# Seven places per dense tile, and a node's own row by a one on the counts' diagonal

## The chip, the cores and the metric

The kernel runs on one core of a Trainium2 chip. The metric is the device time of one execution in microseconds (us). A core has five engines that run their own instruction streams in order and wait for each other by semaphores: TensorE (PE, with its weight loads shown apart as PEld), VectorE (DVE), ScalarE (ACT), GpSimd (POOL) and SyncE (SP, which issues DMAs).

## The reference

The program is one block of a graph network on 6250 nodes with 256 features and 200000 edges, sorted by destination. Cut to what matters here:

```python
xn = _layernorm(x)
# graph convolution: self-loops and symmetric norm
src, dst = concat([A[0], loop]), concat([A[1], loop])     # loop = arange(N): every node's own row
deg  = segment_sum(ones, dst);  dinv = rsqrt(deg)
h    = xn @ W
gnn  = relu(segment_sum(h[src] * (dinv[src] * dinv[dst])[:, None], dst) + b)
# linear attention over all nodes, layer norm, two-layer MLP, layer norm
x = x + gnn + mix(xn)
# top-1 routing to 8 experts with a capacity of 977 tokens, two-layer MLP each
x = x + ffn(_layernorm(x))
```

What bears on the change is the segment sum: for every node the rows of its neighbours, and its own row, are added up.

## The kernel before

The nodes lie in 49 tiles of 128. A first stage (to about 250 us) normalises x, makes the table of rows `h * dinv` (kept on chip as 49 tiles of 128 x 512, a high part and a rest of 256 columns each, and in memory as `g_dram`) and finds the edge lists. The last stage (from about 1150 us) is the experts' MLP. Between them lies the stage that the change rewrites. It runs under an order written out by hand: every engine executes its instructions in the order in which the program writes them. Three generators are stepped in turn.

**Dense tiles (`dense`, letter d).** For 32 of the tiles (`DTS`) the sum over neighbours is a full matrix product: a matrix A of 6272 x 128 counts (how many edges go from each source node to each destination) is multiplied with the whole table. A tile goes through three steps:

1. *Counts.* The tile's destinations are cut into 44 groups of three nodes (the last four groups: two nodes). For each group VectorE makes two one-hot matrices in bf16, `lo` (128 edges x 128 low parts of the source) and `hi` (128 edges x 147 columns, 49 blocks of three nodes), in `onehots` (L1134). TensorE multiplies them (L1177) into a PSUM bank `bp`, and ScalarE writes the bank as bytes into `A` (L1181; the narrow groups by L1184).
2. *Widening.* ScalarE widens some of the 49 source blocks of A to f32r, into `A_r` (L1165, `widened`). `A_r` has two buffers.
3. *The product.* TensorE multiplies every block with its table tile (L1199) and adds all up in one bank `ps_d`. Two products come first: an identity with the tile's own table rows (L1195, the self-loop), and `ohl` with the few left-over edges (L1196). ScalarE and VectorE put the sum away (`put_sum` L1121, `put_rest` L1126).

A tile has `half = NG // 4 = 11` places. In place p the product of tile u-1 takes a tenth of the blocks (p from 1), the one-hots of place p+1 of tile u are made, the next tenth is widened, and the counts of place p-1 are multiplied (four groups in two banks, L1177) and evicted (two evictions). In place 0 there is no product; in place 1 the counts come first.

**Gathered tiles (`gather`, letter g).** For the other 17 tiles the edges' rows are gathered from memory by GpSimd, 128 at a time (L1230, 561 gathers, nine buffers), and summed by a one-hot product (L1256) into `ps`. VectorE makes those one-hots `oh` four steps ahead (L1245), `ohg` once a tile (L1242).

**Rounds (`rounds`, letter s).** Everything else on a pair of tiles: attention, norms, MLP, and three rounds later routing. A plan puts each operation into a numbered slot: `at(k, f, ...)`. A round has `SLOTS_A_ROUND = 14` slots, and successive rounds overlap. Seven operations take one of three PSUM banks named `mm` (`bank()`, pool `mps` with three buffers): `attend` (L1453), `turn` (L295, as `mix_turn` and `slot_turn`), `first` (L1496), `second` (L1514), `gate` (L1422) and routing (L1311). A bank is given back by the operation that reads it: `attended` on VectorE (L1461 to L1466), `mix_turned` and `slot_turned` on ScalarE, `gelu` on ScalarE (L1504), `mixed`, `put_logits` and routing's next step on VectorE. With the pools of `ps` (2), `ps_d` (1) and `bp` (2) the eight banks are all given out.

The main loop steps them: one place of d, then as many slots of s as are due (about 1.01 per place), then as many steps of g as are due (about 1.6 per place). There are 33 x 11 = 363 places.

Of the kernel before, what the change touches and what calls it, by code (L numbers as in the profile page):

```python
# [8 lines left out]
BF16 = mybir.dt.bfloat16  # L9
# [46 lines left out]
SLOTS_A_ROUND = 14  # L56
S_RATE = 1.0104
S_LATE = 6
G_EARLY = 8
# [16 lines left out]
def graph_block_kernel(  # L76
# [127 lines left out]
    V.tensor_scalar(identr, jp, 0.0, None, op0=OP.is_equal)  # L204
    upto = const.tile([P, P], F32, name="upto")
# [12 lines left out]

    Z.tensor_scalar(upto, jp, 0.0, None, op0=OP.is_ge)
# [892 lines left out]
    with tc.manual_schedule():  # L1112
# [16 lines left out]
        def onehots(lists, p):  # L1129

            o = []
            for h, (name, row, w) in enumerate((("lo", rowb, P), ("hi", hib, HW))):
                one = de.tile([P, 4, w], BF16, name=name, tag=name, bufs=3)
                V.tensor_tensor(one.rearrange("p g (w t) -> p g w t", t=2),  # L1134
                                row.rearrange("p (w t) -> p w t", t=2).unsqueeze(1).to_broadcast([P, 4, w // 2, 2]),
                                lists[:, h, 4 * p:4 * p + 4, :].unsqueeze(2).to_broadcast([P, 4, w // 2, 2]),
                                op=OP.is_equal)
                o.append(one)
            return o

# [11 lines left out]
        def dense():  # L1152
# [3 lines left out]
            half = NG // 4  # L1156

            def share(p):
                return (p - 1) * NB // (half - 1), p * NB // (half - 1)

            def widened(u, p):

                s0, s1 = share(p)
                o = parts[p] = de.tile([P, 5, P], FR, name="A_r", tag="A_r")
                nc.scalar.copy(o[:, :s1 - s0, :], mats[u][:, s0:s1, :])  # L1165
# [3 lines left out]
            def counted():  # L1169
                if made and made[0][:2] < (u, p):  # L1170
                    uu, pp, (lo, hi) = made.pop(0)
                    for i in range(2):
                        g = 4 * pp + 2 * i
                        bp = bps.tile([P, 512], F32, name="bp", tag="bp")
                        both = bp[:, :2 * NB * GN].rearrange("p (s k) -> p s k", k=2 * GN)
                        for h in range(2):
                            nc.tensor.matmul(both[:, :, h * GN:(h + 1) * GN], lo[:, 2 * i + h, :],  # L1177
                                             hi[:, 2 * i + h, :NB * GN].rearrange("p (s k) -> p s k", k=GN),
                                             start=True, stop=True)
                        if g < NL:  # L1180
                            nc.scalar.copy(mats[uu][:, :, GN * g:GN * (g + 2)], both)  # L1181
                        else:
                            at = GN * NL + 2 * (g - NL)
                            nc.scalar.copy(mats[uu][:, :, at:at + 4].rearrange("p s (g k) -> p s g k", g=2),  # L1184
                                           both.rearrange("p s (g k) -> p s g k", g=2)[:, :, :, :2])

            for u in range(ND + 1):
                for p in range(half):
                    if p == 1:
                        counted()  # L1190
                    if u >= 1 and p >= 1:

                        if p == 1:
                            acc_ps = dps.tile([P, 2 * D], F32, name="ps_d", tag="ps_d")
                            nc.tensor.matmul(acc_ps, identr, source(DTS[u - 1]), start=True, stop=False)  # L1195
                            nc.tensor.matmul(acc_ps, ohl, left, start=False, stop=False)  # L1196
                        A, (s0, s1) = parts.pop(p), share(p)
                        for hi in range(s0, s1):
                            nc.tensor.matmul(acc_ps, A[:, hi - s0, :], source(hi), start=False, stop=(hi == NB - 1))  # L1199
# [10 lines left out]
                    if u >= 1 and 0 < p < half - 1:  # L1210
                        widened(u - 1, p + 1)
                    if u < ND and p == half - 3:
                        ohl = de.tile([P, P], FR, name="ohl", tag="ohl", bufs=1)
                        V.tensor_scalar(ohl, rowb, dsub[:, DTS[u]:DTS[u] + 1], None, op0=OP.is_equal)
# [5 lines left out]
                    if u >= 1 and p == 0:  # L1220
                        widened(u - 1, 1)
# [122 lines left out]
        def rounds():  # L1344
# [211 lines left out]
            for a in range(NGR):  # L1556
                k = S_ * a - (2 if a == NGR - 1 else 0)
                at(k - 9 if a else 0, load, a)
                at(k + 2, scaled, a)
                at(k + 2, attend, a, 0)  # L1560
                at(k + 4, attend, a, 1)
                at(k + 3, attended, a, 0)
                at(k + 5, attended, a, 1)
                at(k + 7, mix_stats, a, 0)
                at(k + 10, mix_norm, a, 0, (0, 1))
                at(k + 12, mix_turn, a)
                at(k + 13, mix_turned, a)
                at(k + 13, gained, a)
                k += S_
                at(k, first, a)  # L1570
                at(k + 1, gelu, a)
                at(k + 3, second, a)
                at(k + 4, mixed, a)
                if a == NGR - 1:
                    break
                at(k + (5 if a == NGR - 2 else 6), mix_stats, a, 2)
                at(k + 11, mix_norm, a, 2, (0, 1))
                at(k + 11, shift, a)
                at(k + 13, gain, a)
                at(k + 14, joined, a)  # L1580
            for c, r in takes.items():
                k = S_ * r - (2 if c == TAILC - 1 else 0)
                needs[k - 2] = c
                at(k - 2, add_bias, c)
                at(k + 1, to_slot, c)
                at(k + 2, slot_stats, c, 4)
                at(k + 12, slot_norm, c, 4)
                at(k + 13, slot_turn, c)
                at(k + 14, slot_turned, c)
                at(k + 15, gate, c)  # L1590
# [9 lines left out]
                at(k + 16, put_logits)  # L1600
                if c % 2:
# [5 lines left out]
                    at(k + 17, begin)  # L1607
                    soon = (18, 19, 19, 21, 21, 22, 23, 23, 24, 24)
                    sooner = (18, 22, 23, 24, 25, 26, 27, 27, 28, 28)
                    for d in soon if c == TAILC - 1 else sooner if c == TAILC - 3 else (18, 24, 25, 27, 28, 29, 30, 30, 31, 32):  # L1610
                        at(k + d, lambda c=c: walk(batches[c - 1][1]))
            for r in range(NGR):
                at(S_ * r + (6 if r == NGR - 1 else 8), start_roots)
                at(S_ * r + (7 if r == NGR - 1 else 9), end_roots)
# [60 lines left out]
            needs[z + 15], needs[z + 17], needs[z + 25] = b1, b0, b2  # L1675
            for k, f, *args in (
                    (10, enough),
                    (15, add_bias, b1), (15, to_sum, b1, 4),
                    (16, mix_stats, last, 2), (17, add_bias, b0), (17, to_sum, b0, 0),
                    (18, start_roots), (19, end_roots),  # L1680
                    (20, mix_norm, last, 2, (0, 1)), (20, filled, b1, 4), (21, filled, b0, 0),
                    (22, stored, b1), (22, stored, b0), (22, tail_lists, b0),
                    (22, gain, last), (22, shift, last), (22, joined, last),
                    (25, lead, 3), (25, add_bias, b2), (25, to_sum, b2, 0), (25, stored, b2), (25, all_roots),
                    (25, slot_turn, b1), (25, slot_turned, b1), (25, slot_turn, b0), (25, lead), (25, slot_turned, b0),
                    (25, gate, b1), (25, gate, b0), (25, tail_logits, b0, b0, 0), (25, tail_logits, b1, b0, 2),
                    (25, tail_routing, b0, [b0, b1]), (25, go, b0, 2),
                    (26, filled, b2, 0), (26, lead), (26, slot_turn, b2), (26, slot_turned, b2),
                    (26, go, b0, 3), (26, lead), (26, gate, b2),
                    (27, tail_lists, b2), (27, tail_logits, b2, b2, 0), (27, tail_routing, b2, [b2]), (27, go, b2, 2),  # L1690
                    (27, go, b0, 6), (27, lead), (28, go, b2, 2), (28, lead, 2), (28, go, b2, 2), (28, told),
                    (28, go, b2, 20), (28, lead, 30)):
                at(z + k, f, *args)
# [11 lines left out]
        n_dense = (ND + 1) * (NG // 4)  # L1705
        ahead = NG // 4
# [12 lines left out]

        g_rate = (NGT + LAG - 0.8 * ahead) / (n_dense - G_EARLY - ahead)  # L1720
        s_end = SLOTS_A_ROUND * (len(twos) - 1) + 25
        begun, early_in = [], False
        for n in range(n_dense + 1):
# [15 lines left out]
            while counts["g"] < 0.8 * min(n + 1, ahead) + max(0, n + 1 - ahead) * g_rate and step("g"):  # L1739
                pass  # L1740
# [220 lines left out]
```

## Time and profile before

| what | value |
|---|---|
| time, median of 3 runs | 1500.9 us (1500.37 to 1501.51) |
| the profiled execution | 1500.0 us, span 1498.2 us |
| granted TensorE clock, mean | 0.979 |
| dense stage | first count at 248.4 us, last dense product at 1146.2 us |
| PE, DVE, ACT, POOL busy from 270 to 1122 us | 817.6, 675.7, 617.0, 618.8 of 852 us |

The page gives busy time per engine and groups of instructions: line, engine, operation, output and inputs, shapes, count, then busy time and the mean ns of one, then the idle time just before them and what ended it. Matmuls are pipelined, so the mean of one is a latency, and the distance between two starts is what one costs. In a row of waits the numbers are the total in us, how often, and the longest.

### The profile page before, as it was taken

The page shows a single profiled execution, that of the slowest core. Times are in us where ns is not written, and L with a number is a line of the kernel's source. Part 1 is how long each engine was busy: PE and PEld are TensorE (multiplying, and loading weights), DVE is VectorE, ACT ScalarE, POOL GpSimd, SP SyncE. Part 2 cuts the span into 40 slices and gives each one's busy share as a digit, 9 for nine tenths or more (in the row PEclk, how much of TensorE's full clock was granted, in tenths as well). Part 3 has the DMA queues.
Part 4 walks back from the last instruction along what each step waited for, and adds up shares of the span by engine and source line. Part 5 has one row for each costly group of instructions (what it writes and reads, how often), then busy time and mean ns, then how long its engine had stood idle before and what let it go on. Part 6 is the DMA issues. An engine that isn't in the chain of part 4 may idle for free. (4 is left out here: it accounts for less than half of the span.)

```text
span 1498.2 us, 22383 instructions
## 1 busy us (share of the span) xinstructions
PE 1397.7 (93%) x7002; PEld 1020.9 (68%) x7002; DVE 1004.2 (67%) x3435; ACT 900.1 (60%) x2051; POOL 745.3 (50%) x725
## 2 busy tenths in 40 slices
PE   5998997999998999999999989999997999999996
PEld 2665664777776777777776767767775767766854
DVE  6787696678887887878888878888865322222322
ACT  2776564677776777677776767777674333333321
POOL 0101542777776677777766677777661201111111
PEclk9999998999999999999999999999998999999998
DMA  8438675877787777877777777777765343333130
GB/s 266 144 124 275 195 233 172 225 198 201 188 219 207 180 201 211 223 200 214 204 202 205 196 192 202 186 209 210 182 170 171 120 149 110 127 129 132 47 109 11
DMA packets 173459, 267.52 MB, mean 179 GB/s; under 512 B 26409, under 2 KB 73984, under 8 KB 173318
## 3 DMA queue, kind: packets, MB, share of 16 engines
q0 software_dynamic: 89168, 166.39, 42.7%
q1 hardware_dynamic: 83268, 98.39, 19.9%
q10 hardware_dynamic: 882, 1.05, 0.3%
q8 instruction: 65, 1.06, 0.3%
q14 instruction: 76, 0.62, 0.1%
HBM read 208.05 MB, written 60.39 MB: 179 GB/s over the span
## 5 line engine op out<-in xcount | busy, mean ns | idle before, releaser
L1230 POOL DMA_INDIRECT gt<-g_dram,idxc x561 | 592.9, 1057 | 217.1 <-PE ps L1256 79.7
L1199 PE MATMUL ps_d<-tab,A_r 128*128 128x512 f32 x1568 | 425.8, 401 | 10.2 <-ACT A_r L1165 9.9
L1199 PEld LDWEIGHTS ps_d<-tab,A_r 128*128 128x128 f32 x1568 | 292.7, 190 | 88.6 <-ACT A_r L1165 26.5
L1181 ACT CAST A<-bp 128x294 uint8<-128x294 f32 x640 | 237.2, 430 | 186.9 <-PE bp L1177 185.4
L1165 ACT CAST A_r<-A 128x640 fp32r<-128x640 uint8 (+1 forms) x320 | 230.7, 723 | 6.6 <-PE ps_d L1199 5.0
L1256 PE MATMUL ps<-gt,oh 128*128 128x512 f32 x561 | 220.4, 451 | 2.5 <-DVE oh L1245 2.5
L1177 PE MATMUL bp<-hi,lo 128*128 128x147 bf16 x1408 | 187.3, 264 | 22.0 <-DVE hi L1134 13.1
L1177 PEld LDWEIGHTS <-lo 128*128 128x128 bf16 x1408 | 105.0, 105 | 123.0 <-issue 49.3
L1838 POOL DMA_INDIRECT out<-rep,who x43 | 42.5, 989 | 279.4 <-DVE rep L1835 225.5
L1804 PE MATMUL hpf<-xet,w1e 128*128 128x128 f32 (+3 forms) x576 | 159.2, 434 | 8.2 <-ACTq L1916 3.5
L1134 DVE TENSOR_TENSOR lo<-rowb,two 128x512 bf16<-128x512 bf16 x352 | 147.4, 419 | 21.0 <-PE bp L1177 13.6
L1134 DVE TENSOR_TENSOR hi<-hib,two 128x592 bf16<-128x592 bf16 x352 | 161.5, 459 | 0.0
L1814 PE MATMUL ypf<-w2e,hm 128*128 128x256 f32 (+1 forms) x688 | 151.4, 379 | 0.0
L1814 PEld LDWEIGHTS ypf<-w2e,hm 128*128 128x128 f32 (+1 forms) x688 | 128.8, 188 | 21.6 <-issue 2.6
L1245 DVE TENSOR_TENSOR oh<-rowb,rel 128x256 fp32r<-128x256 bf16 x281 | 116.2, 414 | 40.8 <-PE ps L1256 40.2
L1804 PEld LDWEIGHTS hpf<-xet,w1e 128*128 128x128 f32 x576 | 92.6, 198 | 66.4 <-issue 55.7
L1806 ACT ACTIVATE hm<-hpf,fb_s 128x128 f32<-128x128 f32 (+3 forms) x144 | 72.3, 513 | 87.6 <-PE hpf L1804 84.8
L1816 DVE TENSOR_TENSOR y<-ypf,fb_s 128x256 f32<-128x256 f32 (+1 forms) x43 | 18.2, 423 | 130.6 <-PE ypf L1814 130.6
L1256 PEld LDWEIGHTS ps<-gt,oh 128*128 128x128 f32 x561 | 97.2, 195 | 7.9 <-DVE oh L1245 3.4
L1817 ACT ACTIVATE y<-y,xe 128x256 f32<-128x256 f32 (+1 forms) x43 | 21.8, 508 | 124.8 <-DVE y L1816 124.8
L892 PE MATMUL mm<-wqkv_s,xnt 128*128 128x512 f32 (+1 forms) x196 | 93.4, 599 | 0.3 <-DVE tab L481 0.3
L1337 POOL DMA_INDIRECT xbuf<-slot,put x46 | 48.0, 1044 | 58.2 <-issue 29.5
(376 smaller groups left out, 1993.3 us busy)
## 6 DMA issues: line engine op xcount, KB each, us to landing
g_dram<-tab SPq DMA_DIRECT2D x24, 512.0 KB
xbuf<-zeros SPq DMA_DIRECT2D x26, 384.0 KB
gt<-g_dram,idxc POOLq DMA_INDIRECT x561, 3.8
w1e<-in_fw SPq DMA_DIRECT2D x8, 1024.0 KB
w2e<-in_fw SPq DMA_DIRECT2D x8, 1024.0 KB
xe<-xbuf SPq DMA_DIRECT2D x7, 1028.0 KB
xt<-in_x SPq DMA_DIRECT2D x28, 256.0 KB
xe<-xbuf SPq DMA_DIRECT2D x9, 771.0 KB
```

What stands on the lines that cost most here:

```text
L892: nc.tensor.matmul(kp[:r, :], xnt[:, c, i * r:i * r + r], wqkv_s[:, c, D:3 * D], start=(c == 0), stop=(c == 1))
L1134: V.tensor_tensor(one.rearrange("p g (w t) -> p g w t", t=2), row.rearrange("p (w t) -> p w t", t=2).unsqueeze(1).to_broadcast([P, 4, w // ...
L1165: nc.scalar.copy(o[:, :s1 - s0, :], mats[u][:, s0:s1, :])
L1177: nc.tensor.matmul(both[:, :, h * GN:(h + 1) * GN], lo[:, 2 * i + h, :], hi[:, 2 * i + h, :NB * GN].rearrange("p (s k) -> p s k", k=GN), s ...
L1181: nc.scalar.copy(mats[uu][:, :, GN * g:GN * (g + 2)], both)
L1199: nc.tensor.matmul(acc_ps, A[:, hi - s0, :], source(hi), start=False, stop=(hi == NB - 1))
L1230: nc.gpsimd.indirect_dma_start(out=gt, out_offset=None, in_=g_dram, in_offset=bass.IndirectOffsetOnAxis(ap=idxs[j // P][:, j % P:j % P + 1 ...
L1245: V.tensor_tensor(oh, rowb.unsqueeze(1).to_broadcast([P, 2, P]), rel[:, m:m + 2].unsqueeze(2).to_broadcast([P, 2, P]), op=OP.is_equal)
L1256: nc.tensor.matmul(ps, ohs.pop(i), tiles.pop(i), start=False, stop=(e == EB - 1))
L1804: nc.tensor.matmul(hp[:, :nn], w1e[:, c, f * P:(f + 1) * P], xet[:, c, at:at + nn], start=(c == 0), stop=(c == 1))
L1806: nc.scalar.activation(hm[:, f, :nn], hp[:, :nn], AF.Relu, bias=fb1_s[:, e * 8 + f:e * 8 + f + 1])
L1814: nc.tensor.matmul(yp[:r, :], hm[:, f, (i - i0) * P:(i - i0) * P + r], w2e[:, f, :], start=(f == 0), stop=(f == FF - 1))
```

## The change

A dense tile gets seven places for eleven. A place makes and multiplies six groups (two banks of three groups, 441 columns each); the last place has eight, as two banks of two wide and two narrow groups, and the narrow ones are multiplied with their 98 columns alone. `lo` and `hi` have two buffers of six groups, where they had three of four. The blocks are widened in twelve chunks of four or five, two per place, in an order that begins half-way around from the tile's own block. The identity product is gone: in place 2 VectorE adds an identity of bytes, made once at the start, to the counts' own block. A round has nine slots for fourteen, each operation has a new slot, and the due times of the generators are set anew; the gathers get more steps in place 0. There are 33 x 7 = 231 places.

```diff
-SLOTS_A_ROUND = 14
-S_RATE = 1.0104
-S_LATE = 6
-G_EARLY = 8
+PLACES = 7
+CHUNKS = 12
+SLOTS_A_ROUND = 9
+S_RATE = 1.022
+S_LATE = 4
+G_EARLY = 5
+G_FIRST = 1.6
...
+    ident8 = const.tile([P, P], U8, name="ident8")
+    Z.tensor_copy(ident8, ident)
...
-                one = de.tile([P, 4, w], BF16, name=name, tag=name, bufs=3)
+                for g0, n, tag in ((6 * p, 6, name), (6 * PLACES, NG - 6 * PLACES, name + "2"))[:1 + (p == PLACES - 1)]:
+                    one = de.tile([P, n, w], BF16, name=name, tag=tag, bufs=2 if n == 6 else 1)
...
+        def banks_of(p):
+            g = 6 * p
+            if p < PLACES - 1:
+                return [[(g, 3)], [(g + 3, 3)]]
+            return [[(g, 2), (NL, 2)], [(g + 2, 2), (NL + 2, 2)]]
...
-            half = NG // 4
+            half = PLACES
+            def share(u, i):
+                own = next(c for c in range(CHUNKS) if DTS[u] < (c + 1) * NB // CHUNKS)
+                c = (own + i - CHUNKS // 2) % CHUNKS
+                return c * NB // CHUNKS, (c + 1) * NB // CHUNKS
...
                         if p == 1:
                             acc_ps = dps.tile([P, 2 * D], F32, name="ps_d", tag="ps_d")
-                            nc.tensor.matmul(acc_ps, identr, source(DTS[u - 1]), start=True, stop=False)
-                            nc.tensor.matmul(acc_ps, ohl, left, start=False, stop=False)
-                        A, (s0, s1) = parts.pop(p), share(p)
-                        for hi in range(s0, s1):
-                            nc.tensor.matmul(acc_ps, A[:, hi - s0, :], source(hi), start=False, stop=(hi == NB - 1))
+                            nc.tensor.matmul(acc_ps, ohl, left, start=True, stop=False)
+                        for c in (2 * p - 2, 2 * p - 1):
+                            A, (s0, s1) = parts.pop(c), share(u - 1, c)
+                            for hi in range(s0, s1):
+                                nc.tensor.matmul(acc_ps, A[:, hi - s0, :], source(hi), start=False, stop=(c == CHUNKS - 1 and hi == s1 - 1))
+                    if u >= 1 and p == 2:
+                        own = mats[u - 1][:, DTS[u - 1], :]
+                        V.tensor_tensor(own, own, ident8, op=OP.add)
...
-                        widened(u - 1, p + 1)
+                        widened(u - 1, 2 * p)
+                        widened(u - 1, 2 * p + 1)
...
-                k = S_ * a - (2 if a == NGR - 1 else 0)
-                at(k - 9 if a else 0, load, a)
-                at(k + 2, scaled, a)
-                at(k + 2, attend, a, 0)
-                at(k + 4, attend, a, 1)
-                at(k + 3, attended, a, 0)
-                at(k + 5, attended, a, 1)
-                at(k + 7, mix_stats, a, 0)
-                at(k + 10, mix_norm, a, 0, (0, 1))
-                at(k + 12, mix_turn, a)
-                at(k + 13, mix_turned, a)
-                k += S_
-                at(k, first, a)
-                at(k + 1, gelu, a)
+                e = int(a == NGR - 1)
+                k = S_ * a - e
+                at(k - 6 if a else 0, load, a)
+                at(k + 1, scaled, a)
+                at(k, attend, a, 0)
+                at(k + 2, attend, a, 1)
+                at(k + 2, attended, a, 0)
+                at(k + 3, attended, a, 1)
+                at(k + 4, mix_stats, a, 0)
+                at(k + 6, mix_norm, a, 0, (0, 1))
+                at(k + 7, mix_turn, a)
+                at(k + 8, mix_turned, a)
+                k += S_ - (e or a == NGR - 2)
+                at(k + 1, first, a)
+                at(k + 2, gelu, a)
                 at(k + 3, second, a)
                 at(k + 4, mixed, a)
...
-                at(k + 12, slot_norm, c, 4)
-                at(k + 13, slot_turn, c)
-                at(k + 14, slot_turned, c)
-                at(k + 15, gate, c)
+                for d, f in zip((6, 7, 8, 9) if end else (7, 9, 10, 11), (slot_norm, slot_turn, slot_turned, gate)):
+                    at(k + d, f, c, *([4] if f is slot_norm else []))
...
-                at(k + 16, put_logits)
+                at(k + (10 if end else 12), put_logits)
-                    at(k + 17, begin)
+                    at(k + (11 if end else 13), begin)
-                    for d in soon if c == TAILC - 1 else sooner if c == TAILC - 3 else (18, 24, 25, 27, 28, 29, 30, 30, 31, 32):
+                    for d in soon if end else (13, 15, 16, 17, 18, 18, 19, 19, 20, 20):
                         at(k + d, lambda c=c: walk(batches[c - 1][1]))
...
-        g_rate = (NGT + LAG - 0.8 * ahead) / (n_dense - G_EARLY - ahead)
+        g_start = 1.25
+        g_rate = (NGT + LAG - g_start * ahead) / (n_dense - G_EARLY - ahead)
+        def g_due(n):
+            if n < ahead:
+                return g_start * (n + 1)
+            u, p = divmod(n - ahead, PLACES)
+            return g_start * ahead + g_rate * (PLACES * u + G_FIRST + p * (PLACES - G_FIRST) / (PLACES - 1))
```

In the plan, k is nine times the round's number for a, and for c (whose routing lags by three rounds) nine times its taking round; the last rounds have slots of their own.

## The prediction

> **What bounds the kernel now.** I read the page's engine shares first, then the stage windows, then PE's waits inside the dense stage, then the groups, then a few lines of the timeline. A change of about 3 us (0.2%) is what a measurement of this kernel can tell from no change.
>
> ```profile
> PE 1397.7 (93%) x7002; PEld 1020.9 (68%) x7002; DVE 1004.2 (67%) x3435; ACT 900.1 (60%) x2051; POOL 745.3 (50%) x725
> ```
>
> The share is highest on PE, but it is an average over stages. The windows show the stage that is changed (busy us of PE, PEld, DVE, ACT, POOL; clock; DMA share; GB/s):
>
> ```profile
> 270.00:1122.00 852.00, 817.62 (x4500) 610.52 (x4498) 675.70 (x2257) 617.04 (x1391) 618.75 (x586) 0.99 0.77 201
> ```
>
> From 270 to 1122 us PE is busy 817.6 of 852 us at a clock of 0.99; 34.4 us are idle. DVE has 176 us to spare, ACT 235 and POOL 233. So whatever PE is spared, and whatever makes PE wait, goes nearly one to one into the time. PE's waits in that window say how little is left to win there:
>
> ```profile
> PE ps_d L1199 <- ACT A_r L1165: 9.2, 13, 1.6
> PE ps L1255 <- DVE ohg L1242: 6.7, 5, 2.8
> PE bp L1177 <- DVE hi L1134: 5.1, 7, 1.3
> PE bp L1177 <- ACT A L1184: 5.1, 7, 1.1
> PE bp L1177 <- ACT A L1181: 2.0, 7, 0.3
> ```
>
> What is missing counts as much: no matmul into a bank called mm waits for a bank to come free. Three such banks serve attend, turn, first, second, gate and routing.
>
> ```profile
> L1199 PE MATMUL ps_d<-tab,A_r 128*128 128x512 f32 x1568 | 425.8, 401 | 10.2 <-ACT A_r L1165 9.9
> L1177 PE MATMUL bp<-hi,lo 128*128 128x147 bf16 x1408 | 187.3, 264 | 22.0 <-DVE hi L1134 13.1
> L1195 PE MATMUL ps_d<-tab,ident 128*128 128x512 f32 x32 | 15.6, 489 | 0.0
> ```
>
> The mean of one is a latency; matmuls overlap. What a matmul costs PE is the distance to the next start, which the timeline gives:
>
> ```profile
> 713.44 1.32 PE L1199 MATMUL ps_d<-tab,A_r 128*128 128x512 f32 x5
> 714.60 0.51 PE L1177 MATMUL bp<-hi,lo 128*128 128x147 bf16 x4
> 714.89 0.48 PE L1256 MATMUL ps<-gt,oh 128*128 128x512 f32 x1
> 715.21 1.33 PE L1199 MATMUL ps_d<-tab,A_r 128*128 128x512 f32 x5
> ```
>
> Five dense products take 714.60 - 713.44 = 1.16 us, 0.232 each. Four counting products take 0.29 us, and the one f32 product behind them 0.32 instead of 0.232. Single records of the trace: 0.085 from one count to the next, 0.042 from the last count to the f32 product, 0.316 from that to its successor, 0.234 between dense products.
>
> **Part 1, the identity product.** 32 products of L1195 go, one per dense tile. The left-over product then stands first behind the counts and inherits the longer 0.316, so each saves 0.234: 32 x 0.234 = 7.5 us on PE, the path. Its price is 32 adds of 128x128 bytes on VectorE. No such row exists; the nearest are ohl of 128x128 (0.278) and the 128x8 add (0.167): 32 x 0.167 to 0.278 = 5 to 9 us on an engine with 176 us to spare. The add is issued in place 2, the slice with the node's own row is widened in place 3, so ACT finds it done: nothing.
>
> **Part 2, seven places for eleven.** The 44 counts per tile stay, in 7 blocks for 11. A block of n costs (n-1) x 0.085 + 0.042, and 0.082 on the f32 product behind it: n x 0.085 + 0.039. Four blocks fewer: 32 x 4 x 0.039 = 5.0 us. The last four groups shrink from 147 to 98 columns (128 products). In rows, 128 columns against 147 is not shown for these operands; the weight load of L1177 is 0.105 long and the step 0.085. So between 0 (the load sets the step) and a third, 128 x 0.028 = 3.6 us; I take 0, since the 0.085 is nearer to the load.
> "TensorE: Matmul & The Clock Gate" (the Trainium skill, section "Wait — 56ns, not 53.3ns?") gives a warm step of columns over 2.4 GHz plus 2.5 ns. That would be 64 ns for 147 columns against the 85 measured here, and 21 ns less for 98, so an estimate by that page is a saving of 2.7 us.
>
> ACT: 16 evictions per tile for 22. From 196 columns at 0.323 (median) to 294 at 0.416 the slope is 0.95 ns a column, so 441 take 0.56: 12 x 0.56 + 2 x 0.416 + 2 x 0.323 = 8.2 us for 9.0. Widening: 11 x 0.62 + 0.73 = 7.5 for 7.2. DVE: 7 x 1.26 + 0.5 = 9.3 us of one-hots per tile for 11 x 0.878 = 9.7. Neither is on the path; both gains are worth nothing.
>
> **Part 3, waits that come with it.** Two rings change. (a) A_r still has two buffers, but a place now writes two: the first waits for this place's first chunk on PE, the second for its last. Behind them on ACT stand the evictions and the round's work, so ACT starts a round's slot about 0.6 us later, behind PE's dense part. (b) lo and hi have two buffers for three, and three are alive. So VectorE's one-hots wait for this place's counts on PE, and its slot work comes 1.3 us later still. Both results are needed on PE a place (3.9 us) later, which covers them.
>
> **Part 4, nine slots a round for fourteen.** Here I count the mm banks slot by slot. Before, the gate stands in slot 1 (15 mod 14), with only first's bank alive: slot_turn's and routing's are free. After, modulo nine: attend 0 holds a bank from slot 0 to 2, first from 1 to 2, attend 1 takes the third in slot 2, and the gate (k+11, also slot 2) comes behind it. Its bank must come from gelu (ACT) or attended 0 (VectorE) of that same slot. So PE waits in mid-slot for an engine that trails it; gathers and the next dense place are queued behind. How far they trail, the trace shows, since gelu and gate share slot 1 today:
>
> ```profile
> 732.89 0.99 PE L1422 MATMUL mm<-gate_s,xmt 128*128 128x8 f32 x8
> 733.74 1.28 ACT L1504 ACT_TABLE_LOAD   x1
> 735.04 0.84 ACT L1504 ACTIVATE ht<-mm,b_s 128x256 f32<-128x256 f32 x2
> ```
>
> Here gelu ends at 735.88, 2.99 us after the gate began. Over the 22 such pairs of the trace it is 0.68 to 3.1, mean 2.1 us. In the new slot PE has attend 1 to do first, 0.45 us by L1453's steps: 1.65 us. VectorE's way is no shorter: 1.3 of one-hots and 1.25 of attended (L1461 to L1466) from the end of the counts, less 0.45, is 2.1. Gates of c = 0 to 19 meet it; the last rounds are spread otherwise. 20 x 1.65 = 33 us, between 20 x (0.68 - 0.45) = 5 and 20 x (3.1 - 0.45 + 0.6) = 65. I take 33, the mean of the rows for just this pair.
> "Trainium Kernel Development and Optimization" (the Trainium skill, section "Best Practices") says that consistent bubbles can mean that SBUF or PSUM ran out. No row before shows such a bubble; by this count the new slot 2 would.
> "TensorE: Matmul & The Clock Gate" (section "Step-by-step: what each phase is for") says PE pulls only weight loads ahead and keeps matmuls in order, so the wait would hold up everything behind the gate.
>
> **Sum**, against the profiled 1500.0 (span 1498.2, 1.8 around it; 0.9 below the median of the runs): -7.5 - 5.0 + 33 = +20.5, so 1520.5, and 1521 with the 0.9; I take 1520, 1 us off for idle time that such stalls swallow.
>
> **Rivals.** *The banks never decide* (not slower): the point is whether gelu or attended ends before PE reaches the gate. If ACT leads there, the 33 fall away: 1500.9 - 12.5 = 1488; if the fewer places also halve the 21 us of waits for ohg, hi, A and A_r, 1478. For it: ACT idles 185 us before L1181, so it keeps up; in three of 22 pairs gelu trailed by under 0.7. Against: it idles because it waits for PE, so it trails by nature. *VectorE becomes late* (slower still): slot 4 now holds mixed, four statistics, roots and the begin of routing, 4.3 us by their rows, and with one-hots over 6 us for a place of 3.9; the gathers' one-hots, made four steps ahead (2.6 places before, 1.6 now), come late by 1 to 2 us per round: 24 x 1.5 = 36 us instead of or atop: 1540 to 1555. *The change does not do what it says*: the 13 us on PE are hidden by waits that take their place exactly, and the time is the same; PE at 96% leaves little room for it.
>
> **How the numbers follow.** The gate's wait 0.47 (1520, its own 1503 to 1545), VectorE late 0.21 (1530 to 1555), banks never decide 0.28 (1478 to 1494), nothing shown 0.04. Both signs hold chance, so the range reaches from 1480 to 1548. Faster 0.28, same 0.04, slower 0.68.
>
> **What would show it.** Right: no L1195; 16 evictions per tile; a new wait of PE at the gate (L1422) ended by gelu or attended, some 1.7 us and 20 times; PE's busy time in the dense stage down by 12, its idle up by 30. Wrong: no PE wait at L1422, or PE's idle time below 34 us. VectorE late would show as PE waits for oh or hi above 10 us.

## The result, and the profile after

The changed kernel takes 1630.1 us (median of 4 runs, 1624.3 to 1633.4), the kernel before 1501.2 (1500.4 to 1502.1): 1.0854 times as long, 95% interval 1.082 to 1.0888. The forecast had the sign, but +129 us is far from its +19 and lies 82 us above the end of its range. The profiled execution spans 1622.5 us (before 1498.2), so 124.3 us are to be found. The mean granted TensorE clock is 0.941 (before 0.979).

The engine shares of the page, then the window from 270 to 1122 us (busy us of PE, PEld, DVE, ACT, POOL; clock; DMA share; GB/s):

```profile
PE 1433.8 (88%) x6970; PEld 1069.2 (66%) x6970; DVE 1007.8 (62%) x3276; ACT 909.9 (56%) x1923; POOL 727.7 (45%) x725
```

```profile
270.00:1122.00 852.00, 746.16 (x3894) 574.35 (x3892) 593.40 (x1836) 545.27 (x1106) 526.70 (x511) 0.93 0.67 176
```

PE idles 105.8 of 852 us, where it idled 34.4, and the clock in the window is 0.93 for 0.99. Every other engine does less as well: no engine has become a new bound. PE's waits in the dense stage (total us, times, longest):

```profile
PE ps L1284 <- DVE oh L1273: 41.7, 21, 5.4
PE mm L1450 <- ACT ht L1532: 26.1, 13, 3.9
PE mm L1450 <- DVE s L1494: 21.3, 7, 5.1
PE ps L1283 <- DVE ohg L1270: 18.7, 9, 4.0
```

L1450 is the gate (L1422 before). It waits 20 times, as counted: 13 times for gelu's bank (L1532), 7 times for attended's (L1494). But the gathers' one-hots, `oh` and `ohg`, cost more still: 60.4 us. What VectorE waits for itself, first before, then after:

```profile
DVE slot L1390 <- DMA xbuf<-slot,put: 51.4, 9, 9.0
DVE lo L1134 <- PE bp L1177: 13.6, 20, 1.1
```

```profile
DVE lo L1141 <- PE bp L1199: 189.3, 102, 6.4
DVE slot L1418 <- issue: 31.6, 8, 5.2
```

The wait at `to_slot` (L1390, then L1418) is not new: with its smaller rows it is 54 us in 10 waits before and 41 in 10 after, by the row of before for the DMA that reads the slot's buffer. New is the wait for the ring: VectorE makes the next `lo` only when PE's counts have given one of the two buffers back, and everything that stands behind it on VectorE waits too. One case from the timeline of after (start, duration, then idle before and its releaser in brackets):

```profile
818.96 0.56 DVE L1141 TENSOR_TENSOR lo<-rowb,two 128x768 bf16<-128x768 bf16 x1 [2.46 <-PE bp L1199]
...
820.37 0.68 DVE L1551 TENSOR_TENSOR s<-mm,s 128x512 f32<-128x512 f32 x1
...
824.23 0.42 DVE L1273 TENSOR_TENSOR oh<-rowb,rel 128x256 fp32r<-128x256 bf16 x1
...
824.70 0.73 PE L1284 MATMUL ps<-gt,oh 128*128 128x512 f32 x2 [3.92 <-DVE oh L1273]
```

VectorE stands still for 2.46 us for a buffer, then has slot 4's work (mixed at L1551, four statistics, roots) in front of `oh`, and PE stands still for 3.92 us in turn. While PE stands, no counts give a buffer back, so the two delays can feed each other.

The third loss is the clock. Three windows around a gate that waited 1.88 us (from 399.41 to 401.29 us):

```profile
400.00:402.00 2.00, 0.71 (x7) 0.71 (x7) 1.79 (x7) 1.77 (x4) 1.68 (x2) 1.00 1.00 300
402.10:405.50 3.40, 3.40 (x14) 2.69 (x14) 1.00 (x5) 0.57 (x2) 1.83 (x2) 0.50 0.74 219
405.50:409.00 3.50, 3.50 (x15) 2.23 (x14) 2.76 (x9) 1.84 (x3) 1.93 (x3) 1.00 0.76 205
```

After the wait the granted clock is 0.50 for 3.4 us, then 1.00 again. The timeline shows what that does to eight dense products, once at the full clock and once, for the most part at half, behind a gate that waited 5.12 us:

```profile
701.82 2.02 PE L1222 MATMUL ps_d<-tab,A_r 128*128 128x512 f32 x8
...
806.67 1.88 PE L1450 MATMUL mm<-gate_s,xmt 128*128 128x8 f32 x8 [5.12 <-DVE s L1494]
...
809.39 3.08 PE L1222 MATMUL ps_d<-tab,A_r 128*128 128x512 f32 x8
```

I added up PE's records from the first to the last dense product: the distance of each start to the next, less the idle time in front of the next, is a step. I kept apart steps at the full clock, and of the others what they took over the full-clock mean of their kind:

| us in the stage | before | after | difference | the prediction's sum |
|---|---|---|---|---|
| PE steps, at the full clock | 837.5 | 825.9 | -11.6 | -12.5 |
| more on steps at half clock | 7.8 | 52.3 | +44.5 | none |
| PE idle | 39.1 | 126.8 | +87.7 | +33 |
| of it before gathered products and their `ohg` | 9.2 | 62.2 | +53.0 | none |
| of it before rounds' products (gate 47.4 after) | 7.0 | 57.9 | +50.9 | +33 |
| of it before counts and dense products | 22.9 | 6.7 | -16.2 | none |
| the stage | 884.8 | 1005.2 | +120.4 | +20.5 |

The rest, +3.9 us, lies outside the stage. The stage spends 137 us at half clock, before 17.

### The profile page after: what moved, and what is told of

Read it like the earlier page. It is cut to its first block, busy times and chain, and to the rows that moved or that the text cites. A ratio compares the mean times of both kernels' runs of the same rounds, so it can differ in the third digit from the quotient of the medians.

```text
span 1622.5 us, 22398 instructions
## 1 busy us (share of the span) xinstructions
PE 1433.8 (88%) x6970; PEld 1069.2 (66%) x6970; DVE 1007.8 (62%) x3276; ACT 909.9 (56%) x1923; POOL 727.7 (45%) x725
## 5 line engine op out<-in xcount | busy, mean ns | idle before, releaser
L1258 POOL DMA_INDIRECT gt<-g_dram,idxc x561 | 573.9, 1023 | 338.8 <-PE ps L1284 203.5
L1222 PEld LDWEIGHTS ps_d<-tab,A_r 128*128 128x128 f32 x1568 | 313.3, 200 | 84.4 <-ACT A_r L1184 9.2
L1184 ACT CAST A_r<-A 128x512 fp32r<-128x512 uint8 (+1 forms) x384 | 234.3, 627 | 206.6 <-PE ps_d L1222 175.5
L1207 ACT CAST A<-bp 128x441 uint8<-128x441 f32 (+2 forms) x512 | 237.3, 529 | 70.4 <-PE bp L1199 69.2
L1141 DVE TENSOR_TENSOR lo<-rowb,two 128x768 bf16<-128x768 bf16 (+1 forms) x256 | 131.1, 522 | 202.2 <-PE bp L1199 189.3
L1284 PE MATMUL ps<-gt,oh 128*128 128x512 f32 x561 | 210.0, 461 | 43.5 <-DVE oh L1273 41.7
L1199 PE MATMUL bp<-hi,lo 128*128 128x147 bf16 (+1 forms) x1408 | 167.2, 269 | 9.5 <-DVE hi L1141 8.3
L1199 PEld LDWEIGHTS <-lo 128*128 128x128 bf16 x1408 | 114.6, 112 | 76.1 <-issue 53.8
L1141 DVE TENSOR_TENSOR hi<-hib,two 128x888 bf16<-128x888 bf16 (+1 forms) x256 | 145.2, 577 | 0.0
L1284 PEld LDWEIGHTS ps<-gt,oh 128*128 128x128 f32 x561 | 101.8, 204 | 63.7 <-DVE oh L1273 52.7
```

The lines of the kernel that those rows point to most:

```text
L1199: nc.tensor.matmul(both[:, :, at:at + w], lo[g], hi[g][:, :NB * GN].rearrange("p (s k) -> p s k", k=GN)[:, :, :w], start=True, stop=True)
L1207: nc.scalar.copy(mats[uu][:, :, to:to + w * n], both[:, :, at:at + w * n])
L1258: nc.gpsimd.indirect_dma_start(out=gt, out_offset=None, in_=g_dram, in_offset=bass.IndirectOffsetOnAxis(ap=idxs[j // P][:, j % P:j % P + 1 ...
L1284: nc.tensor.matmul(ps, ohs.pop(i), tiles.pop(i), start=False, stop=(e == EB - 1))
```

## The experiments

Edits are to the changed kernel unless said otherwise. All kernels ran beside the kernel before on their chip; its median was 1503.4, 1503.2 and 1502.7 us in the three studies told first. The table gives what the rest of the section reads (us; steps, half clock and idle as in the table above). The time is a median; the other columns are of the one profiled execution, which took 1500.0, 1634.4, 1598.6, 1571.1, 1519.9, 1505.8, 1531.9 and 1523.6 us in the order of the rows, so they go with the medians to within 7 us:

| kernel | time | stage | full-clock steps | more at half clock | PE idle |
|---|---|---|---|---|---|
| before, profiled | 1501.2 | 884.8 | 837.5 | 7.8 | 39.1 |
| after_again | 1633.5 | 1004.9 | 825.5 | 52.4 | 126.8 |
| gate_later_again | 1593.7 | 966.9 | 819.7 | 44.8 | 102.4 |
| counts_first_again | 1577.7 | 947.9 | 821.8 | 32.4 | 93.6 |
| gate_first_ohg_again | 1519.5 | 898.3 | 816.3 | 17.6 | 64.2 |
| all_ahead_nine_rows | 1505.8 | 882.8 | 817.1 | 21.0 | 44.6 |
| before_ring_of_two_again | 1528.0 | 914.0 | 841.7 | 11.9 | 59.7 |
| before_bank_only | 1523.7 | 901.7 | 838.9 | 13.5 | 48.7 |

**The two kernels once more**, as the ground for the others.

> The changed kernel unchanged, beside the kernel before on one chip with the next three. The first study's chip gave the kernel before 1594 us where the first comparison's gave 1501; the changed kernel was not run there. Both theories: 1.085 times the kernel before if the chip is like the first; on one like the second a ratio of 1.03 to 1.05, since gate_later (1.030) and counts_first (1.024) should be under it.

> The kernel before unchanged, for its profile on this chip. On a chip like the first: 1501 us, PE idle about 38 us in the dense stage, under 20 us of it at half clock. On one like the second: 1594 us, with PE waits for counts, evictions and widening some 60 us longer and more half clock.

After: 1633.5 us (1626.4 to 1635.2), ratio 1.0849 (1.0818 to 1.0879). Before, in one run: 1502.3. The waits, the half clock and the steps come out as in the first pair within a few us.

**The gate alone.** It moves one slot back, where a bank is free.

```diff
-  ... zip((6, 7, 8, 9) if end else (7, 9, 10, 11), (slot_norm, slot_turn, slot_turned, gate)):
+  ... zip((6, 7, 8, 9) if end else (7, 9, 10, 12), (slot_norm, slot_turn, slot_turned, gate)):
-                at(k + (10 if end else 12), put_logits)
+                at(k + (10 if end else 13), put_logits)
```

> The changed kernel with gate and put_logits one slot later, on a chip to be compared by its kernel before (1501 to 1503 where the changed kernel took 1630 to 1634). The bank alone: the 48 us of waits at the gate go and a third of the 116 us of extra half clock, so 1565 to 1575. If the waits only move to oh and ohg (60 us, then over 90): over 1600.

1593.7 us, ratio 1.059 (1.0565 to 1.0616): 40 us less than the changed kernel. PE's waits no longer have a line for the gate, but the others grew:

```profile
PE ps L1284 <- DVE oh L1273: 57.4, 26, 5.4
PE ps L1283 <- DVE ohg L1270: 19.5, 10, 4.0
```

47 us of gate waits are gone, and 16.5 of them came back as waits for `oh` and `ohg`: what came late there was hidden behind the gate's wait. Another 5.9 us came back at `second` (L1540), which now waits twice for attended's bank. The time lies between the two forecasts: the bank was a real cost, but not all of it, and not all of its wait was gained.

**The ring alone.** The counts of a place come ahead of its dense products in every place, not only in the second, so the one-hots' buffers come back about 2 us earlier.

```diff
-                    if p == 1:
+                    if p >= 1:
                         counted()
...
-                    if p != 1:
+                    if p == 0:
                         counted()
```

> The changed kernel with the counts multiplied first in every place, the ring of lo and hi given back earlier. The ring alone: waits for oh and ohg fall from 60 to under 25 us, the waits at the gate shrink a little since VectorE is less late, 1575 to 1590. If the ring is not what makes VectorE late: over 1615.

1577.7 us, 1.0498 (1.048 to 1.0515): 56 us less, as forecast, with the gate where it was. VectorE's wait for the ring falls from 189.3 to 70.5 us:

```profile
DVE lo L1141 <- PE bp L1199: 70.5, 74, 5.0
```

PE's gate wait falls with it, from 47.4 to 37.6 us (L1450: 23.5 by attended, 14.1 by gelu), and its waits for `oh` and `ohg` from 60.4 to 45.2. The forecast had these under 25: more than the ring makes them late.

**Both, and `ohg` three steps earlier.**

```diff
-                if i >= 0 and i % EB == 0:
+                if i + 3 >= 0 and (i + 3) % EB == 0 and i + 3 < NGT:
-     ... dsub[:, GTS[i // EB]:GTS[i // EB] + 1] ...
+     ... dsub[:, GTS[(i + 3) // EB]:GTS[(i + 3) // EB] + 1] ...
```

> The gate a slot later, the counts first and ohg earlier, once more, beside the changed kernel. Bank and ring with the half clock that they cause: at least 60 us under the changed kernel on a chip like the first (waits at the gate 47 and for oh and ohg 60 us fall by two thirds, half clock by half). Rival 'the lumped slot 4 and the tight widening ring': under 40 us, with waits for oh and A_r that stay near 50 us.

1519.5 us, 1.0101 (1.0084 to 1.0118): 114 of the 130 us are gone, with the seven places, the wide banks, the ring of two and the diagonal still in. The window:

```profile
270.00:1122.00 852.00, 792.04 (x4370) 613.22 (x4369) 667.84 (x2073) 619.96 (x1246) 605.51 (x577) 0.98 0.76 198
```

Waits for the gate are gone and those for `ohg` are down to 0.5 us; what is left is `oh`, 50.0 us in 28 waits, as the rival expected of the lumped slot 4. So the lump is real too, though the time says that it is the smaller part.

**The ring in the kernel before.** Three buffers of four groups become two, nothing else.

```diff
-                one = de.tile([P, 4, w], BF16, name=name, tag=name, bufs=3)
+                one = de.tile([P, 4, w], BF16, name=name, tag=name, bufs=2)
```

> The kernel before with two buffers for lo and hi where it had three, on a chip like the first. The ring's theory: over 1515, VectorE's waits for counts over 80 us for 13, PE's idle time in the stage over 60 us for 38. If eleven small places cover a ring of two: within 5 us of the kernel before.

1528.0 us, 1.0159 (1.0142 to 1.0176): +25 us from the ring alone, at a gate that never waits for a bank. VectorE's waits, then PE's (13.1, 9.9 and 6.7 us before; 8.1 of the first row's 16.5 stand ahead of the stage):

```profile
DVE lo L1134 <- PE bp L1177: 112.9, 111, 6.0
```

```profile
PE bp L1177 <- DVE hi L1134: 16.5, 11, 8.1
PE ps_d L1199 <- ACT A_r L1165: 14.7, 16, 1.5
PE ps L1255 <- DVE ohg L1242: 14.0, 8, 4.5
```

**The bank in the kernel before.** Both attends move to slot 1, so that with first three banks are held where the gate comes.

```diff
-                at(k + 2, attend, a, 0)
-                at(k + 4, attend, a, 1)
+                at(k + 1, attend, a, 0)
+                at(k + 1, attend, a, 1)
```

> The kernel before with attend 0 and attend 1 both in slot 1, so that the gate of that slot finds all three mm banks held and waits for gelu: the bank's part of the change alone, ring of three, eleven places. The prediction's sum: 22 waits of 2.1 us less the two attends (0.9) is 26 us and nothing else, 1527. Theory that a wait is paid again in half clock: waits of over 1.5 us are followed by 3.4 us at half clock, so the time rises by half as much again as the waits. If earlier ScalarE work hides most: under 10 us in all.

1523.7 us, 1.0135 (1.0099 to 1.0172): +21 us.

```profile
PE mm L1422 <- ACT ht L1504: 21.7, 17, 2.1
```

17 waits of 1.28 us each: the prediction's row, 2.1 us, less two attends of 0.45 instead of one, is 1.2. The waits swallowed 13 us of others, so PE's idle time in the stage is only 9.6 us up on before; half clock adds 5.7, steps 1.4, and 7 us lie outside the stage.

**The diagonal in the kernel before.** The identity product goes, the add comes in place 3, and the shares are turned half-way around.

```diff
-                            nc.tensor.matmul(acc_ps, identr, source(DTS[u - 1]), start=True, stop=False)
-                            nc.tensor.matmul(acc_ps, ohl, left, start=False, stop=False)
+                            nc.tensor.matmul(acc_ps, ohl, left, start=True, stop=False)
...
+                    if u >= 1 and p == 3:
+                        own = mats[u - 1][:, DTS[u - 1], :]
+                        V.tensor_tensor(own, own, ident8, op=OP.add)
```

> The kernel before with one part of the change: the own row by an add on the counts' diagonal in place 3, blocks in an order half-way around from the tile's own, no identity product; eleven places, fourteen slots, three buffers. Theory of the prediction: 32 x 0.234 = 7.5 us less than before and no new wait, 1494 on a chip like the first. Rival: the add makes ScalarE wait at the widening; same or up to 5 us slower.

1507.4 us (10 runs), 1.0028 (1.001 to 1.0047): 4 us slower, where 7.5 less was counted. Here the left-over product takes 0.410 us to its successor at the full clock, where identity (0.318) and left-over (0.234) took 0.552: 0.142 saved each, 4.5 us. The mean hides two cases. In 14 of 31 tiles it is 0.33, as in the changed kernel (0.32). In the other 17 the next product comes 0.54 to 0.65 us later, up to 0.18 of it idle, and starts 0.05 us after ScalarE has ended the first widened chunk:

```profile
479.33 0.73 ACT L1170 CAST A_r<-A 128x640 fp32r<-128x640 uint8 x1
479.57 0.47 PE L1200 MATMUL ps_d<-left,ohl 128*128 128x512 f32 x1
480.11 0.53 PEld L1203 LDWEIGHTS ps_d<-tab,A_r 128*128 128x128 f32 x3 [0.38 <-ACT A_r L1170]
```

In the kernel before, the identity product covered this: there 17 of the 32 first dense products start only 0.05 to 0.17 us after their chunk is ready, and none waits. Without it PE comes to that chunk too early. So the time is the rival's, but the wait is PE's, and the add is not its cause. In the profiled run PE idles 8 to 10 us more than before, but that run took 1514.2 us, 7 over its median.

**`ohg` earlier in the kernel before**, the same edit as above.

> The kernel before with ohg made three steps earlier, nothing else. Its 7 us of waits for ohg go: 1494 to 1497. If something else is late by as much there: 1501 to 1503.

1496.7 us (9 runs), 0.9957 (0.9944 to 0.997): 6 us less, a small gain but clear of the noise. The waits for `ohg` are gone, PE idles 36.2 us in the stage, and half clock falls from 17 to 7 us. The window's clock is 1.00:

```profile
270.00:1122.00 852.00, 820.52 (x4536) 613.10 (x4535) 681.81 (x2274) 621.84 (x1402) 617.58 (x587) 1.00 0.77 201
```

**The one-hots earlier as well**, atop gate, counts and `ohg`. In the first kernel two steps of lead and a buffer of `oh` are paid for with one of the nine gather buffers; in the second with routing's second buffers.

```diff
-AHEAD = 4
+AHEAD = 6
...
-                    oh = ga.tile([P, 2, P], FR, name="oh", tag="oh", bufs=3)
+                    oh = ga.tile([P, 2, P], FR, name="oh", tag="oh", bufs=4)
```

```diff
# all_ahead_six
-GB = 9
+GB = 8
# all_ahead_nine_rows
-                return small([P, 5, N_EXP], name)[:, :m, :]
+                return small([P, 5, N_EXP], name, bufs=1)[:, :m, :]
```

> The gate later, the counts first, ohg earlier, and oh made six steps ahead for four (four buffers for three; the gathered rows have eight for nine). gate_first_ohg took 1519 with 50 us of PE waits for oh left. If those come from the lumps of VectorE's work in slot 4: waits for oh under 15 us, half clock as before the change, 1470 to 1485, faster than the kernel before. If VectorE is late by more than two steps at the lumps, or eight row buffers hold the gathers up: 1500 to 1520.

> As all_ahead_six with nine buffers for gathered rows (three small routing tiles give the room). all_ahead_six had 13 us of PE waits for gathered rows and 10 for oh. If those rows came late for want of the ninth buffer: 1490 to 1500, under the kernel before. If the gathers are late for the burst in place 0: no change from 1510.

1510.4 us, 1.0053 (1.0035 to 1.0072), and 1505.8 us (10 runs), 1.0016 (1.0001 to 1.003). The first came as its rival had it, the second between its two forecasts. With eight gather buffers PE now waits for the gathers themselves; with nine less so:

```profile
PE ps L1284 <- DMA gt<-g_dram,idxc: 13.8, 19, 3.7
PE ps L1284 <- DVE oh L1273: 10.5, 4, 6.1
```

```profile
PE ps L1284 <- DVE oh L1273: 11.3, 4, 5.0
...
PE ps L1284 <- DMA gt<-g_dram,idxc: 8.2, 9, 2.7
```

The stage takes 882.8 us in the second, 2 us less than before: 20.4 saved on full-clock steps, 13.2 given back at half clock, 5.5 in idle time. Outside the stage 8 us are added, so the whole is no faster.

**The same with the identity product back**, and no add.

> As all_ahead_nine_rows, but the identity product is back and the add on the diagonal is gone. The prediction's part 1: 7.5 us slower than all_ahead_nine_rows. By diag_alone, where the left-over product took 0.416 us instead of 0.240 after the identity was gone: 4 to 5 us of PE steps, and not over that in time.

1507.8 us (10 runs, 1496.0 to 1516.3), 1.0028 (1.0001 to 1.0055): 2 us from the kernel with the add, inside the intervals. Full-clock steps differ by 4.4 us; the time can't tell that from nothing.

**A first study on another chip.** Four of these kernels ran earlier, on a chip where the kernel before took 1594.0 us (13 runs).

> The changed kernel with gate and put_logits one slot later, so that the gate finds a bank given back a place before. Theory 'the bank': the 47 us of PE waits at the gate fall under 5 us, about 25 us of PE time at half clock go with them, and the time falls from 1630 to about 1560. Rival 'VectorE late': the gate's wait only stood in front of another; waits for oh and ohg grow from 60 us by as much, and the time stays over 1600.

> The changed kernel with one edit: the counts of place p-1 are multiplied ahead of the products in every place, not behind them, so the two-buffer ring of lo and hi is given back 2 us earlier. Theory 'the ring': VectorE's wait for the counts (189 us) falls under 100, PE's waits for oh and ohg fall from 60 us to under 25, the time to about 1575. Rival 'the bank alone': waits for oh stay, the time stays within 10 us of 1630.

> The gate one slot later, the counts first in every place, and ohg made three steps earlier. If bank and ring are all of it, with the half clock they cause: 1490 to 1515, clock in the dense stage back to 0.98. If something else in the seven places costs (two A_r buffers for two chunks a place, the lumped slot 4): over 1530, with PE waits for A_r or oh above 20 us.

> The kernel before with two buffers of four groups for lo and hi, where it had three: the ring's part of the change alone, in eleven places. Theory 'the ring': VectorE waits for counts over 80 us (13.6 before), PE waits for oh, ohg and hi grow from 14 to over 30 us, the time is 1515 to 1540. Rival 'the ring is covered': within 5 us of 1501, since all those results are needed a place later.

They took 1646.4 (1.030, 1.0225 to 1.0375), 1635.5 (1.0241, 1.0177 to 1.0305), 1603.5 (1.0062, 1.0029 to 1.0095) and 1620.3 us (1.0145, 1.0085 to 1.0206). The order is the same, and the ring costs 26 us there. The instructions of these four lasted as long there as in their repeats, yet their stage was 49 to 84 us longer; of the kernel before there is no trace from there. The four traces lack some four tenths of the semaphore events that would say why. That is left open, and no number of that chip is set against the others.

## Why the prediction was right and wrong, point by point

**Part 1, the identity product: right in steps, not seen in the time.** The add takes 0.282 us, just over the range's upper end of 0.278, and nobody waits for it:

```profile
L1225 DVE TENSOR_TENSOR A<-A,ident x32: 276/282/308, 267.6 to 1254.6; 128x128 uint8<-128x128 uint8 x32
```

At the full clock the left-over product costs 0.321 us for 0.552 with the identity: 0.231 saved each, 7.4 us for 7.5. The pair with and without it at the end of the experiments shows 2 us, less than its runs scatter. In the kernel before, the product had covered a wait for the first widened chunk, a use that the sum did not count: without it 17 tiles run into that wait.

**Part 2, fewer and wider blocks: right in the sum, which is in part luck.** All full-clock steps together fell by 11.6 us for 12.5, and by 16 to 21 in the table's other kernels with seven places and an edit. By kind it looks less exact: counts took 1.6 us less, gathered products 7.9 and dense ones 2.3 less, while attend's products took 6.6 more, which no term foresaw. The narrower counts, put at nothing because the weight load should set the step, were worth some 2 us: from one narrow count to the next it is 0.063 us, where wide ones take 0.085. (The prediction's estimate of 21 ns for this is 20.4 by its own formula, 2.6 us for 2.7; the rows show 22.) The evictions became 16 per tile and cost PE nothing; its waits before counts fell from 12.7 to 0.7 us in the stage:

```profile
L1207 ACT CAST A<-bp 128x441 uint8<-128x441 f32 (+2 forms) x512 | 237.3, 529 | 70.4 <-PE bp L1199 69.2
```

**Part 3, the waits: this step failed.** It said of the late one-hots and slot work: "Both results are needed on PE a place (3.9 us) later, which covers them." The cover counted one delay of 1.3 us. It left out what stands on the same engine in front of the next due result: in the case above 2.46 us of waiting, `lo` and `hi`, then 3.9 us of slot work (820.37 to 824.23) ahead of `oh`. The 60.4 us of waits for `oh` and `ohg` (before 9.2) are the price. The trace of after tells what VectorE did during each of these waits and the 5 us before it. Behind 33 us of them it had stood idle for the ring (over 0.4 us); behind 22 us it had not been idle, so PE waited for the lumped work alone; behind 5 us it had stood at `to_slot`. So the ring is the larger part, and the lump, which only the rival counted, is next. Counts first moves the ring's part, and with it a part of the gate's wait (-56 us); the kernel before with two buffers shows the ring to cost 25 us with all else as it was. In the kernel with gate, counts and `ohg` moved, 3 of the 52 us that are left stand behind the ring, 21 behind work alone, 19 behind `to_slot` and the rest behind `put_rest`. A ring of three in the changed kernel and a further buffer for the slot weren't tried.

**Part 4, the gate's bank: mechanism right, size off.** Twenty waits, by gelu and attended, as counted; 47.4 us for 33, 2.4 each for 1.65. With the ring and the places of before, the same conflict gives 1.28 each, so the rows were read rightly for the kernel in which they stood. In the new kernel the engines behind the bank are themselves late, in every second round above all: eight waits take 30.9 us, the other twelve 1.4 each, under the 1.65 that was counted. In those eight rounds VectorE stands 4 to 5 us at `to_slot` (L1418), as it did before the change, and ScalarE loads a table ahead of gelu (1.28 us); what each adds isn't told apart. In one such case (timeline of after) VectorE waits 4.10 us before `to_slot`, then makes held-back one-hots, and only then ends attended, which gives the bank back:

```profile
641.93 0.17 DVE L1418 CAST slot<-pid 128x2 int32<-128x2 f32 x1 [4.10 <-issue]
...
645.40 1.88 PE L1450 MATMUL mm<-gate_s,xmt 128*128 128x8 f32 x8 [3.85 <-DVE s L1494]
```

The gate alone, moved, was worth 40 us: its wait and clock less what the one-hots and `second` took back.

**The sum: no term for the clock.** 44.5 us of the 120 in the stage are steps at half clock: in this pair 0.5 us more for each microsecond of added idle time. The prediction read 0.99 in the window and asked nothing further. "TensorE: Matmul & The Clock Gate" (the Trainium skill, section "HAM oscillation — how this bites in real kernels") gives as a rule that PE should have no idle gaps over about 3.4 us. The pieces at half clock do come in multiples of 3.41 us here, and all 34 in the trace start whole multiples of 3.413 us apart, but shorter waits are followed by them too: of the idle gaps in the stage of after, a piece of half clock starts within about 3 us of 13 of 14 gaps over 3 us, 9 of 11 from 2 to 3 us, 4 of 10 from 1.5 to 2 us, and 3 of 13 from 1 to 1.5 us. The measurement decides: 17 of these 29 gaps are shorter than 3.41 us.

**The rivals.** "VectorE becomes late" was given 0.21 and 36 us "instead of or atop" the gate. It is what happened, but atop, and at 53 us more than before for `oh` and `ohg`; its reason, the lumped slot 4, is the smaller part beside the ring. The text's own mark, waits for `oh` or `hi` above 10 us, is passed four times over. "The banks never decide" and "nothing shown" fall with the 20 waits. The sum with measured terms: -11.6 (steps), +50.9 (rounds, the gate above all), +53.0 (`oh`, `ohg`), -16.2 (counts and dense products wait less), +44.5 (clock), +3.9 (outside the stage): +124.5, the 124.3 of the two spans within rounding.

**What is not settled.** How the 114 us divide between gate, ring and `ohg`: 40 and 56 are each measured with the other still in, and they feed each other. And why the seven-place kernels lose 4 to 16 us outside the stage, even where the stage is as short as before. The eleven-place edits lose 1 to 7 there, and the changed kernel's own two profiles differ by 10, so part of it is not of the seven places.

## What to carry to other kernels

When tiles get larger and their ring shorter, count for every place which buffers are still alive when the next one is asked for; if all are, the producer is tied to the consumer's pace, and everything queued behind the producer is late with it. Delays of this kind can add up rather than take turns, and where TensorE sets the time its waits cost clock as well: in this pair half a microsecond for each that was waited, in most of the table's other kernels 0.2 to 0.6, and in all_ahead_nine_rows 13 us at only 5.5 us more of idle time. So a tuned order can lose far more than the one wait that was foreseen. Before work is taken off the path, ask also what it covered: the identity product hid a wait for the widening. A small operand that is made just before its use is cheap to make a few steps earlier: `ohg` alone took 6 us off the kernel before.

## What the hardware showed that was not expected

- Half clock after short waits: pieces of 3.41 us or multiples at 0.5, mostly after PE waits over 2 us, on one grid of 3.413 us over the whole trace. At half clock a dense product takes 0.427 us to the next start for 0.235, a count 0.150 for 0.082, a gathered product 0.483 for 0.291.
- The first f32 product behind the bf16 counts takes 0.32 us to its successor where nothing waits; 0.235 is what dense products take among themselves. Where the successor waits for its operand, the distance grows to 0.47 us before any idle time shows.
- The same kernel, before, took 1594 us on one chip and 1501 to 1503 on others. Four other kernels, traced on both, show the same durations of single instructions.
